# Two slots of 160 for an expert's last whole slot and its rest, with a projection and weight loads moved, in a two-layer gated cross-attention kernel

## The chip, the core and the metric

The kernel runs on one core of a Trainium2 chip. The metric is the device time of one execution in microseconds (us). The core's engines work side by side, each on its own in-order queue: TensorE (PE) multiplies, with its weight loads shown as a row of their own (PEld); VectorE (DVE) and ScalarE (ACT) work on elements; GpSimd (POOL) does the rest of the element work and issues the gathers and scatters by index; SyncE (SP) issues nearly all other transfers. Waits between queues go by semaphores. The profile also shows the clock that TensorE was granted, as a share of full speed.

## The reference, cut to what matters

Two layers; each adds a cross-attention and a mixture of experts to x (8 batches of 100 tokens, 512 features). All is float32.

```
x = x + tanh(g_xattn[0]) * L0_xattn(ctx, layernorm(x), mask)
x = x + tanh(g_ffn[0])   * L0_ffn(layernorm(x))
x = x + tanh(g_xattn[1]) * L1_xattn(layernorm(x), ctx)
x = x + tanh(g_ffn[1])   * L1_ffn(layernorm(x))

L0_ffn:  4 experts, 2048 hidden, the two best by softmax probability
    logits = x @ router_w + router_b
    out = sum over the token's experts e of gate[t, e] * (silu(x @ w1[e]) * (x @ w3[e])) @ w2[e]
L1_ffn:  8 experts, 1024 hidden, the two best by logit, gates by their softmax
    the same with W1, W2, W3
```

Layer 0's attention has latents from x and keys and values from a masked context of 722 tokens and the latents; 16 heads of 64. Layer 1's attention reads every 16th key of the context's projection; 16 heads of 32. So 1600 token-expert pairs go through each mixture, and how many fall to each expert is known only when the router has run.

## The kernel before, in words

**Layer 0's attention** has two forms, and the kernel branches between them at run time: `attend_to_all`, and `attend_to_few` where no pair of batches has more than 128 usable context tokens. These inputs take the second, called the arm below. Ahead of the branch run the masks' running counts (`cum`, written to DRAM as `cum_d`) and the first latents; the largest count is read into a register, and each engine branches on it. In the arm, `bring` loads a pair's counts back to all partitions, `find` turns them into row indices on VectorE, `fetch` gathers the context rows, and `Pair.steps` builds queries (`wq`), values (`wv`) and keys (`wk`). The loop over the four pairs weighs one pair's heads (`softmax`, `weigh`, `finish`) and between them runs steps of a list `fill`: the next pair's projections, the earlier pair's output projection, routers, and in the last pair the first half of layer 1's keys and values (`kv`) and the choice of layer 0's first expert (`First.find`, one stage for each `c`). The stages end in 24 tiny matmuls (`pe_f`, L542) that put the first slot's rows in order.

**A mixture** works in slots: one expert's weights times up to 256 tokens. The first slot takes up to 256 tokens of the expert that is most wanted among the early batches (6 of layer 0, 5 of layer 1), so it can start before the router has seen all. Its rows come from `First`: `begin_rows` issues the gathers on POOL, `begin_weights` reads the expert's number into a register of SP and issues the weights, 1 MB each: w1 and w3 (up) and w2 (down) for each group of 512 hidden features; three buffers of each. While the first slot runs, `steps` runs between its products: what is left of the attention (`last_outputs`: the output projections of batches 6 and 7; two steps of it ahead of the slot), the routers of the late batches, and `dispatch`, the plan for all other tokens: counts per expert, minus what the first slot took, cut into whole slots of 256 and a rest. `SLOTS` says how many slots of each size there are: `(n_mid, n128, always, n256, middle)`. A rest of at most 128 goes into one of the n128 slots, one up to `middle` (192 in layer 0, 160 in layer 1) into one of the n_mid, a larger one into a whole slot, and so does whatever no longer fits. The first `always` whole slots run unconditionally, further ones each behind a branch. The order is: middle slots, slots of 128, whole slots. `slot` multiplies with w1 and w3 (L1564), gates on ScalarE and VectorE, and multiplies with w2, turned for a middle slot (L1536, results transposed back in the next slot, L1601) and straight for the others (L1547); `before_last` transposes the next slot's gathered rows (L1510) between the last two down products.

**Layer 1's attention** runs batch by batch; its router of a batch follows one batch behind (`route`), and `First.find` runs its stages in the last two batches. `mix.begin_weights(2)` loads w1 and w3 as soon as the expert is known; the rest follows at the end of the loop.

The code is traced in program order; a scheduler then orders each engine's queue by what is ready in its own estimate, and adds the semaphores. `issue_after` holds the instructions of its block behind one instruction on that one's engine.

Of the kernel before, what the change touches and what calls it, by code (L numbers as in the profile page):

```python
# [42 lines left out]

WHOLE = 2 * P
# [4 lines left out]
SLOTS1 = (2, 4, 3, (2 * NT - 2 * EARLY1 * S // E1 + E1 * (WHOLE - 1)) // WHOLE, 160)  # L49
# [14 lines left out]
def flamingo_gated(  # L64
# [84 lines left out]
    def load_kv0(pool, bufs, order):  # L149

        wkv_r = wkv0.rearrange("(kc p) n -> p kc n", p=P)
        tiles = {}
        for k, i in enumerate(order):
            t = pool.tile([P, KC, 512], FP, tag=("wk", "wv")[i // 2], name="wkv", bufs=bufs)
            nc.sync.dma_start(t, wkv_r[:, :, bass.ts(i, 512)])
            tiles[i] = t
            if k == 1:
                load_x(2, 3)
        return [tiles[0], tiles[1]], [tiles[2], tiles[3]]
# [101 lines left out]
    with ExitStack() as ph:  # L261
        ps_c = ph.enter_context(tc.tile_pool(name="p_ps", bufs=1, space=PSUM))
        nc.vector.tensor_copy(cum, m8)

        nc.vector.tensor_tensor_scan(cum, cum, cum, 0.0, ALU.add, ALU.max)
        pm = ps_c.tile([1, 512], FP, name="pm")
        nc.tensor.transpose(
            pm[:, :PAIRS], cum[:, 2 * CTX - 1 : 2 * CTX], ident[:PAIRS, :PAIRS]
        )
        top = prep.tile([1, 1], FP, name="top")  # L270
        nc.vector.tensor_reduce(top, pm[:, :PAIRS], AX.X, ALU.max)
        nc.vector.tensor_copy(most, top)
        nc.gpsimd.dma_start(cum_d, cum)
    prep.release()
# [18 lines left out]
    def project_out(b, ps, tag, work, y_tag="y", y_bufs=1):  # L293
        oT = oT0[:, :, bass.ts(b % 2, S)]
        py = ps.tile([P, 512], FP, tag=tag, name="py")
        for c in range(IN0 // P):
            nc.tensor.matmul(
                py[:S],
                oT[:, c, :],
                wo[:, c, :],  # L300
                start=(c == 0),
                stop=(c == IN0 // P - 1),
            )
        add_normed(b, py, work, y_tag, y_bufs)

# [164 lines left out]
    class First:  # L470
# [3 lines left out]
        def __init__(self, E, early, lg, gates, t_gate):  # L474
            self.E, self.early, self.lg, self.gates, self.t_gate = E, early, lg, gates, t_gate
            self.rows = state.tile([P, 2], I32, name=f"f_rows{E}")
            self.gate = state.tile([P, 2], FP, name=f"f_gate{E}")
            self.e = state.tile([1, 1], I32, name=f"f_e{E}")
            self.taken = state.tile([P, E], FP, name=f"f_taken{E}")

        def find(self, space, ps, tag):
# [58 lines left out]
            for t in range(2):  # L540
                for k in range(b):
                    nc.tensor.matmul(  # L542
                        pe[:, bass.ts(t, 2)], place[:, k, bass.ts(t, P)], what[:, k],
                        start=(k == 0), stop=(k == b - 1),
                    )
# [7 lines left out]
            v.scalar_tensor_tensor(self.rows, both[:, :, 0], -1.0, free, ALU.add, ALU.add)  # L553
# [47 lines left out]
    def load_heads(pool):  # L601
# [4 lines left out]
        def load(c, kc):  # L606
            if kc < 2:
                t = pool.tile([P, KC, 512], FP, tag="wv", name="ch", bufs=2)
# [11 lines left out]
    def attend_to_all():  # L620
# [210 lines left out]
        wk, wv = load_kv0(kvp, 2, (0, 1, 2, 3))  # L831
# [3 lines left out]
        for b in range(B):  # L835
# [5 lines left out]
            for hf in range(2):  # L841
# [16 lines left out]
                if hf == 0:  # L858
                    v = v_next
            if b < EARLY0:  # L860
                project_out(b, ps_mm, "mm", work, "o", 2)
# [4 lines left out]
        for _, step in keys_values_1(  # L866
# [7 lines left out]
            load_heads(kvp),  # L874
# [5 lines left out]
    def attend_to_few():  # L880
# [264 lines left out]
        space = bring(0, pair.kT)  # L1145
        wk, wv = load_kv0(kvp, 2, (2, 3, 0, 1))
        load_rest()
        find(0, space)
        pair.fetch()
        pair.norm_context()  # L1150
        for k, (_, step) in enumerate(pair.steps()):
# [13 lines left out]
            load_heads(kvp),  # L1165
# [3 lines left out]
        for i in range(PAIRS):  # L1169
# [11 lines left out]
            else:  # L1181
# [6 lines left out]
                fill += [c, kv[3], kv[4], c, c, kv[5], c, c, kv[6], c, kv[7], c]  # L1188
# [19 lines left out]
            for c in range(n):  # L1208
                now = softmax(pair, c)
                while done < len(fill) and cost < whole * (c + 1) / n:  # L1210
# [5 lines left out]
                last = now  # L1216
            finish(*last)
# [39 lines left out]
    def dispatch(E, slots, first, wk_, ps_pool):  # L1257
# [6 lines left out]
        n = base + 2 * n256  # L1264
        v = nc.vector
# [52 lines left out]
        v.tensor_tensor(put[:, 0], put[:, 0], put[:, 1], ALU.subtract)  # L1318
        ends = vec("ends", 3)
# [4 lines left out]
        for k, have in ((0, n_mid), (1, n128)):  # L1324
# [3 lines left out]
            v.tensor_tensor(put[:, k], put[:, k], fit[:, 0], ALU.mult)  # L1328
        apart = vec("apart")
        v.tensor_tensor(apart[:, 0], put[:, 0], put[:, 1], ALU.add)  # L1330
        yield
# [9 lines left out]
        v.tensor_scalar(rest[:, 0], ends[:, 0], 2.0, -2.0, ALU.mult, ALU.add)  # L1341
        v.tensor_tensor(rest[:, 0], rest[:, 0], put[:, 0], ALU.mult)
# [27 lines left out]
        v.tensor_tensor(far, far, grid(main), ALU.add)  # L1370
        v.tensor_tensor(at2[:, 0], at2[:, 0], far, ALU.add)
        yield
# [73 lines left out]
    class Mixture:  # L1446
# [38 lines left out]
        def begin_weights(self, upto=3):  # L1485

            if not self.w0:
                self.e = self.expert(self.first.e[0:1, 0:1])
# [233 lines left out]
    def last_outputs(ps, work):  # L1722
        for b in range(EARLY0, B):
# [29 lines left out]
    mix.run(last_outputs, range(EARLY0, B), 2, 1, between, ending)  # L1753
# [5 lines left out]
    with ExitStack() as ph:  # L1759
# [161 lines left out]
        for b in range(B):  # L1921
# [5 lines left out]
            if b:  # L1927
                logits = route(
                    b - 1, ps_t, "t", wk_, wg, lg1, out, nc.scalar.copy, nc.sync
                )  # L1930
# [8 lines left out]
            project_1(b, oT)  # L1939
# [86 lines left out]
```

## Time and profile before

| what | us |
|---|---|
| median of 3 runs (1433.77 to 1436.92) | 1436.36 |
| the profiled execution | 1435.67 |
| its span, first to last instruction | 1433.9 |
| the branch is left on POOL, VectorE (first instruction behind it) | 16.96, 20.11 |
| first queries, first values on PE | 17.44, 33.57 |
| last weighing in layer 0's attention ends | 390.97 |
| first product of layer 0's first slot | 415.21 |
| first product of layer 1's first slot | 1098.90 |
| first slot of 160, of 128, of 256 of layer 1 begins | 1148.76, 1204.85, 1292.56 |
| last product ends | 1418.4 |

The span is cut on the page into 40 slices of 35.85 us. Page rows give an engine's busy share; a row of the timeline reads: start, length, engine, line, operation, output<-inputs, shapes, count, and in brackets the engine's idle time just before and what released it ("issue": nothing that the profile shows). The mean granted clock is 0.982 over the span.

### The profile page before, as it was taken

How to read it: one execution, taken by the hardware profiler on the slowest of the kernel's cores; microseconds unless marked ns; L12 is line 12 of the kernel's file. 1: busy time of each engine (PE TensorE's matmuls, PEld its weight loads, DVE VectorE, ACT ScalarE, POOL GpSimd, SP SyncE). 2: the span in 40 equal slices, each digit the busy share in tenths (PEclk: the TensorE clock that was granted, in tenths of full speed). 3: DMA queues.
4: the chain of work that ended last, by engine and by line, in shares of the span. 5: the costliest groups of instructions: out<-in, count | busy, mean ns of one | idle time of the engine just before them, and what ended most of it. 6: DMA issues, size and time to landing. Idle time of an engine off the chain costs nothing. (4 is left out here: it accounts for less than half of the span.)

```text
span 1433.9 us, 18211 instructions
## 1 busy us (share of the span) xinstructions
PE 1371.5 (96%) x7077; PEld 1024.5 (71%) x7077; DVE 479.4 (33%) x1357; ACT 251.7 (18%) x727; POOL 185.5 (13%) x277
## 2 busy tenths in 40 slices
PE   4999999999999999999999999998998999999995
PEld 3566857767568699997677777764666799787773
DVE  4353654535735121222121212113574423222220
ACT  1124423234311000100000000002542001010000
POOL 3410201100120100010000000005211111110000
PEclk9999999999999999999999999998997999999998
DMA  8400101111296466664355526422015578885521
GB/s 274 128 1 0 41 6 35 60 33 44 106 334 235 140 218 226 205 221 157 125 170 176 191 91 218 138 83 62 24 47 213 220 265 270 292 304 194 191 45 17
DMA packets 103856, 207.95 MB, mean 145 GB/s; under 512 B 6166, under 2 KB 13338, under 8 KB 103748
## 3 DMA queue, kind: packets, MB, share of 16 engines
q1 hardware_dynamic: 95556, 186.72, 37.1%
q0 software_dynamic: 8192, 19.84, 5.7%
q8 instruction: 61, 1.00, 0.3%
q14 instruction: 47, 0.39, 0.1%
HBM read 191.18 MB, written 15.36 MB: 144 GB/s over the span
## 5 line engine op out<-in xcount | busy, mean ns | idle before, releaser
L1564 PE MATMUL pa<-xTs,w 128*128 128x256 f32 (+3 forms) x1536 | 317.3, 349 | 1.4 <-DVE xTs L1513 1.3
L1564 PE MATMUL pb<-xTs,w 128*128 128x256 f32 (+3 forms) x1536 | 312.9, 347 | 0.0
L1564 PEld LDWEIGHTS pa<-xTs,w 128*128 128x128 f32 x1536 | 262.5, 191 | 33.9 <-issue 9.9
L1564 PEld LDWEIGHTS pb<-xTs,w 128*128 128x128 f32 x1536 | 262.6, 191 | 22.8
L1547 PE MATMUL py_e<-w,hT 128*128 128x512 f32 x512 | 225.7, 593 | 0.0
L1572 ACT ACTIVATE sg<-pa 128x256 f32<-128x256 f32 (+3 forms) x192 | 67.2, 350 | 718.6 <-PE pa L1564 708.9
L1573 DVE TENSOR_TENSOR sg<-sg,pa 128x256 f32<-128x256 f32 (+3 forms) x192 | 72.9, 380 | 345.8 <-ACT sg L1572 345.8
L1547 PEld LDWEIGHTS py_e<-w,hT 128*128 128x128 f32 x512 | 96.2, 191 | 106.4 <-issue 103.6
L1574 DVE TENSOR_TENSOR hT<-sg,pb 128x256 f32<-128x256 f32 (+3 forms) x192 | 72.8, 379 | 124.6 <-PE pb L1564 124.4
L1052 PE MATMUL pv_f<-wkv,kvT 128*100 128x512 f32 (+1 forms) x192 | 87.8, 607 | 3.4 <-DVE qT L1029 3.4
L1038 PE MATMUL pk_f<-kvT,wkv 128*128 128x328 f32 x256 | 73.3, 444 | 1.1 <-ACT kvT L1009 1.0
L1472 POOL DMA_INDIRECT xt<-xnd,rows x26 | 25.5, 982 | 373.6 <-PE pt_s L1510 293.5
L1052 PEld LDWEIGHTS pv_f<-wkv,kvT 128*100 128x100 f32 (+1 forms) x192 | 33.3, 177 | 48.6 <-issue 43.7
L1090 ACT ACTIVATE pr_f<-pr_f,nmax 100x228 f32<-100x228 f32 x128 | 60.7, 475 | 36.5 <-DVE nmax L1080 33.1
L1038 PEld LDWEIGHTS pk_f<-kvT,wkv 128*128 128x128 f32 x256 | 47.9, 190 | 23.9 <-ACT kvT L1009 2.1
L1080 DVE CUSTOM_DVE_ANT_0 pr_f<-ps_sf,bias 100x228 f32<-100x228 f32 x128 | 43.7, 391 | 54.3 <-PE ps_sf L1067 54.1
L1536 PE MATMUL py_e<-hT,w 128*128 128x192 f32 (+1 forms) x384 | 61.0, 318 | 0.0
L1536 PEld LDWEIGHTS py_e<-hT,w 128*128 128x128 f32 x384 | 59.3, 190 | 0.0
L1606 POOL DMA_INDIRECT xr<-ye,rows x12 | 18.7, 1559 | 267.5 <-DVE ye L1605 266.9
L1022 PE MATMUL pq_f<-kvT,wq 128*128 128x200 f32 x256 | 46.4, 342 | 3.0 <-ACT kvT L1009 3.0
L1513 DVE COPY xTs<-pt_s 128x512 f32<-128x512 f32 x30 | 19.7, 687 | 86.7 <-PE pt_s L1510 86.7
L1022 PEld LDWEIGHTS pq_f<-kvT,wq 128*128 128x128 f32 x256 | 44.3, 195 | 4.3 <-ACT kvT L1009 4.0
(353 smaller groups left out, 1203.2 us busy)
## 6 DMA issues: line engine op xcount, KB each, us to landing
w<-in_f_w_dram SPq DMA_DIRECT2D x144, 1024.0 KB
ch<-in_ctx_heads_dram SPq DMA_DIRECT2D x12, 720.0 KB
wkv<-in_wkv_dram SPq DMA_DIRECT2D x4, 1024.0 KB
kT<-cum_d SPq DMA_DIRECT2D x4, 722.0 KB
wq<-in_ctx_heads_dram SPq DMA_DIRECT2D x4, 720.0 KB
wq<-in_wq_dram SPq DMA_DIRECT2D x4, 512.0 KB
wo<-in_wo_dram SPq DMA_DIRECT2D x1, 2048.0 KB
xnd<-xn POOLq DMA_DIRECT2D x9, 200.0 KB, 4.6
```

Of the source, the lines that this page charges most:

```text
L1022: nc.tensor.matmul(pq[:, bass.ts(i, 2 * S)].rearrange("p (j s) -> p j s", j=2), wq[:, kc, bass.ts(c0 + i, P)], self.lats[kc], start=(kc == 0),
L1038: nc.tensor.matmul(pk[:, : S + FK], wk[c // 4][:, kc, bass.ts(c % 4, P)], self.kvT[:, kc], start=(kc == 0), stop=(kc == KC - 1),)
L1052: nc.tensor.matmul(pv[:n], self.kvT[:, kc, k0 : k0 + n], wv[hf][:, kc, :], start=(kc == 0), stop=(kc == KC - 1),)
L1080: nc.vector.tensor_tensor_reduce(out=pr[:, r, j], in0=ps[:S, r, bass.ts(j, FK)], in1=p.bias[j], scale=-1.0, scalar=FMAX, op0=ALU.add, op1= ...
L1090: nc.scalar.activation(pr[:, r, j], pr[:, r, j], AF.Exp, bias=nmax, scale=-1.0, accum_out=sm[:, r, j : j + 1],)
L1472: nc.gpsimd.indirect_dma_start(out=xt, out_offset=None, in_=xnd[: LEAD + upto * S], in_offset=bass.IndirectOffsetOnAxis(ap=rows[:, k : k + ...
L1536: nc.tensor.matmul(pys[c // 2][:, bass.ts(c % 2, T)], w2[:, i, bass.ts(c, P)], hT[:, i, :T], start=False, stop=(fg == F // FG - 1 and i == ...
L1547: nc.tensor.matmul(py[:n], hT[:, i, c : c + n], w2[:, i, :], start=(fg == 0 and i == 0), stop=(fg == F // FG - 1 and i == FG // P - 1),)
L1564: nc.tensor.matmul(p[:, :T], w[:, kc, bass.ts(i, P)], xT[:, kc, :T], start=(kc == 0), stop=(kc == KC - 1),)
L1572: nc.scalar.activation(sg[:, :T], pa[:, :T], AF.Sigmoid)
L1573: nc.vector.tensor_tensor(sg[:, :T], sg[:, :T], pa[:, :T], ALU.mult)
L1574: nc.vector.tensor_tensor(hT[:, i, :T], sg[:, :T], pb[:, :T], ALU.mult)
```

## The change

It has six parts.

- `SLOTS1` is (4, 3, 2, n256, 160) instead of (2, 4, 3, n256, 160), and `dispatch` learns to split: where an expert has a whole slot and a rest of at most 2 x (middle - 128) tokens (64 in layer 1, 128 in layer 0) and two middle slots are free, its last whole slot and the rest go into two middle slots. It costs some VectorE operations and one more stage.
- The output projection of batch 6 leaves the mixture's first slot and goes into the arms. In the arm of these inputs `project_parts` cuts it at chunks 3 and 6: the first piece before the last stage but one of the choice, the second before the last head pair is finished, the third behind it. Of the stages one call less stands in `fill`; the rest of the choice runs behind the third piece. The mixture runs one step instead of two ahead of its first slot.
- The two value weights of layer 0's attention (`wv`) and the first pair's running counts (into `wo`'s space, `cum0`) are loaded ahead of the branch, in the order wv0, cum0, wv1; then, inside the arm, the first pair's `find` and `fetch`, the two `wk`, x of batches 2 and 3, and the rest.
- The first slot's expert number is copied a second time (`e_late`) behind its rows, and the second `begin_weights` of layer 1 reads that copy.
- In the last batch of layer 1's attention the rows of batch 6 are normalized first; router 6 and projection 7 go behind the last of the choice's tiny matmuls (`counted`) on PE.
- Layer 1's chunk loads take the `wv` tiles themselves instead of new tiles of that tag.

```diff
-SLOTS1 = (2, 4, 3, (2 * NT - 2 * EARLY1 * S // E1 + E1 * (WHOLE - 1)) // WHOLE, 160)
+SLOTS1 = (4, 3, 2, (2 * NT - 2 * EARLY1 * S // E1 + E1 * (WHOLE - 1)) // WHOLE, 160)
...
+    def load_kv0(pool, tag, i, bufs=1):
+
+        t = pool.tile([P, KC, 512], FP, tag=tag, name="wkv", bufs=bufs)
+        nc.sync.dma_start(t, wkv_r[:, :, bass.ts(i, 512)])
+        return t
...
         nc.gpsimd.dma_start(cum_d, cum)
+
+        cum0 = wo.rearrange("p c n -> p (c n)")[:, : 2 * CTX]
+        wv = [load_kv0(wpool, "wv0", 2)]
+        nc.sync.dma_start(cum0, cum_d[0].partition_broadcast(P))
+        wv.append(load_kv0(wpool, "wv1", 3))
     prep.release()
     few = nc.values_load(most, min_val=0, max_val=2 * CTX)
...
+    def project_parts(b, cuts, ps, tag, work, y_tag="y", y_bufs=1):
+
+        n = IN0 // P
         py = ps.tile([P, 512], FP, tag=tag, name="py")
-        for c in range(IN0 // P):
+        for c in range(n):
+            if c in cuts:
+                yield
             nc.tensor.matmul(
...
-            v.scalar_tensor_tensor(self.rows, both[:, :, 0], -1.0, free, ALU.add, ALU.add)
+            known = v.scalar_tensor_tensor(
+                self.rows, both[:, :, 0], -1.0, free, ALU.add, ALU.add
+            )
+            with tc.issue_after(known.ins):
+                v.tensor_copy(self.e_late, number)
...
         pair = Pair(0)
-        space = bring(0, pair.kT)
-        wk, wv = load_kv0(kvp, 2, (2, 3, 0, 1))
+        find(0, cum0)
+        pair.fetch()
+        wk = [load_kv0(kvp, "wk", i, 2) for i in range(2)]
+        load_x(2, 3)
         load_rest()
-        find(0, space)
-        pair.fetch()
...
-                fill += [c, kv[3], kv[4], c, c, kv[5], c, c, kv[6], c, kv[7], c]
+                fill += [c, kv[3], kv[4], c, c, kv[5], c, kv[6], c, kv[7], c]
...
                 now = softmax(pair, c)
-                while done < len(fill) and cost < whole * (c + 1) / n:
+                if following is None and c == n - 1:
+
+                    parts = project_parts(EARLY0, (3, n - 2), ps_mm, "mm", work)
+                    fill.insert(-1, (0, lambda: next(parts)))
+                while done < len(fill) and (cost < whole * (c + 1) / n or c == n - 1):
...
+            if following is None:
+                next(parts)
+                finish(*last)
+                next(parts, None)
+                for _ in choice:
+                    pass
+                break
...
+        over_ = middle - P
...
+        two = vec("two")
+        v.tensor_scalar(two[:, 0], left[:, 0], float(2 * over_), None, ALU.is_le)
+        v.tensor_tensor(two[:, 0], two[:, 0], some[:, 0], ALU.mult)
+        had = vec("had")
+        v.tensor_scalar(had[:, 0], q[:, 0], 0.0, None, ALU.is_gt)
+        v.tensor_tensor(two[:, 0], two[:, 0], had[:, 0], ALU.mult)
+        v.scalar_tensor_tensor(put[:, 0], two[:, 0], 2.0, put[:, 0], ALU.mult, ALU.add)
...
+            if not k:
+                v.tensor_tensor(two[:, 0], two[:, 0], fit[:, 0], ALU.mult)
+                v.tensor_tensor(put[:, 1], put[:, 1], two[:, 0], ALU.subtract)
+                v.tensor_tensor(q, q, two, ALU.subtract)
         apart = vec("apart")
         v.tensor_tensor(apart[:, 0], put[:, 0], put[:, 1], ALU.add)
+        v.tensor_tensor(apart, apart, two, ALU.subtract)
...
+        yield
+        v.scalar_tensor_tensor(row, grid(q), -2.0, at2[:, 0], ALU.mult, ALU.add)
         v.tensor_tensor(at2[:, 0], at2[:, 0], far, ALU.add)
+        turns = wk_.tile([S, 2, B, E], FP, tag="pick", name="turns")
+        for t in range(2):
+            v.tensor_scalar(turns[:, t], row, float(1 + t), None, ALU.is_equal)
+            v.tensor_tensor(turns[:, t], turns[:, t], grid(two), ALU.mult)
+        v.tensor_tensor(at2[:, 0], at2[:, 0], turns[:, 0], ALU.add)
+        v.tensor_tensor(at2[:, 0], at2[:, 0], turns[:, 1], ALU.subtract)
+        v.tensor_scalar(row, at2[:, 1], float(over_), None, ALU.is_ge)
+        v.tensor_tensor(row, row, turns[:, 1], ALU.mult)
+        v.scalar_tensor_tensor(at2[:, 0], row, 2.0, at2[:, 0], ALU.mult, ALU.add)
+        v.scalar_tensor_tensor(at2[:, 1], row, -float(over_), at2[:, 1], ALU.mult, ALU.add)
...
-            if not self.w0:
-                self.e = self.expert(self.first.e[0:1, 0:1])
+            self.e = self.expert((self.first.e_late if self.w0 else self.first.e)[0:1, 0:1])
...
-        for b in range(EARLY0, B):
+        for b in range(EARLY0 + 1, B):
             project_out(b, ps, "m", work)
...
-    mix.run(last_outputs, range(EARLY0, B), 2, 1, between, ending)
+    mix.run(last_outputs, range(EARLY0, B), 1, 1, between, ending)
...
-            if b:
-                logits = route(
-                    b - 1, ps_t, "t", wk_, wg, lg1, out, nc.scalar.copy, nc.sync
-                )
+            how = (ps_t, "t", wk_, wg, lg1, out, nc.scalar.copy, nc.sync)
+            if b > EARLY1 + 1:
+                xn = norm_rows(b - 1, wk_, out, nc.sync)
+            elif b:
+                logits = route(b - 1, *how)
...
                 next(find)
-            project_1(b, oT)
+                with tc.issue_after(first1.counted.ins):
+                    logits = route(b - 1, *how, xn)
+                    project_1(b, oT)
+            else:
+                project_1(b, oT)
```

## The prediction

> **What bounds the kernel now.** First the page's busy times and its slices: is one engine full, and where not.
>
> ```profile
> span 1433.9 us, 18211 instructions
> PE 1371.5 (96%) x7077; PEld 1024.5 (71%) x7077; DVE 479.4 (33%) x1357; ACT 251.7 (18%) x727; POOL 185.5 (13%) x277
> ...
> PE   4999999999999999999999999998998999999995
> ```
>
> TensorE (PE) is full but for the two ends and a dip near slice 28. Time can be won by giving PE less to do, or at its few waits. Then the stretches of layer 1's slots, cut where the chain of waits changes from one slot to the next; each row gives a stretch's length, busy times, granted clock, DMA share and GB/s:
>
> ```profile
> 1148.76:1176.58 27.82, 27.82 (x203) 27.18 (x203) 7.18 (x19) 2.85 (x9) 3.57 (x3) 1.00 0.70 230
> 1176.58:1204.85 28.27, 28.27 (x209) 27.76 (x209) 7.72 (x20) 2.85 (x9) 3.99 (x3) 1.00 0.75 246
> 1204.85:1227.32 22.47, 22.47 (x158) 18.56 (x158) 7.19 (x20) 2.22 (x8) 3.91 (x3) 1.00 0.85 294
> 1227.32:1248.92 21.60, 21.60 (x151) 17.74 (x150) 6.06 (x18) 2.22 (x8) 2.57 (x2) 1.00 0.91 316
> ...
> 1334.79:1377.03 42.24, 42.24 (x170) 31.30 (x169) 9.53 (x20) 3.06 (x8) 3.08 (x2) 1.00 0.44 134
> ```
>
> Two slots of 160, two of 128, one of 256: PE is busy throughout, so a slot's length is its PE work. Last the timeline at the seams, where PE waits. Around the end of layer 0's attention arm:
>
> ```profile
> 387.00 0.56 PE L1122 MATMUL po_f<-cT,v 128*64 128x200 f32 x4 [1.67 <-ACT cT L1119]
> ...
> 390.90 5.28 PE L542 MATMUL pe_f<-space 100*128 100x2 f32 x24
> ...
> 396.54 15.38 PE L297 MATMUL py<-wo,oT 128*100 128x512 f32 x32 [0.35 <-DVE space L548]
> ...
> 411.75 0.60 PE L1510 MATMUL pt_s<-ident,xt 128*128 128x128 f32 x4
> ```
>
> and at the start of layer 1's mixture:
>
> ```profile
> 1085.59 2.31 PE L542 MATMUL pe_f<-xT 100*128 100x2 f32 x20
> ...
> 1088.78 1.10 POOL L1472 DMA_INDIRECT xt<-xnd,f_rows  x1 [4.29 <-DMA w<-in_f_w_dram]
> ...
> 1095.36 1.09 PE L1510 MATMUL pt_s<-ident,xt 128*128 128x128 f32 x4 [3.82 <-DMA xt<-xnd,f_rows]
> ...
> 1098.90 3.78 PE L1564 MATMUL pa<-xTs,w 128*128 128x256 f32 x8
> ```
>
> At the first seam PE goes straight on into the two late output projections (py, 32 matmuls); at the second it waits 3.82 us for the gathered rows, and its first 8 products then take 3.78 us, where later ones take 1.73.
>
> **Part 1, the slots.** Which slots run hangs on the data. Evaluating the reference's second router on its inputs gives 239, 98, 255, 130, 129, 125, 294 and 330 tokens for the eight experts; the first slot takes 225 of the last, leaving 105. Today that is two slots of 160 (130, 129), four of 128 (98, 125, 105, and the 38 behind 294's whole slot) and three of 256 (239, 255, 294): the sizes that the trace shows, with nothing in the conditional slots. After, the 294 go into two of 160 (256 + 38, and 38 is under 64): four of 160, three of 128, two of 256, again exactly what is unconditional. Added: two slots of 160. One that follows and precedes another costs 28.27 + 0.43 (it turns two gathered tiles for its successor, where the row's slot turns one; four transposes are half of the 0.87 us that eight take) = 28.70. Taken away: 21.60 and 42.24. So 2 x 28.70 - 21.60 - 42.24 = **-6.4 us**. The slots load as many weights as before, nine times 6 MB; the longest run of short ones becomes three of 128 (DMA share 0.91 in such a slot) where it was four, so DMA does not step in. Layer 0's counts (186, 253, 162, 231 left, two of them behind a whole slot) call for no split: its slots stay.
>
> **Part 2, the plan costs more VectorE work.** About 11 narrow operations (128x8) and 11 wide (100x64) come in, and the plan is asked for one step later. In the first slot 54 such operations took 6.0 us (1111.14 to 1117.16), 0.11 each; a wide one that waits for its predecessor took about 0.24 (L1369 at 1116.32, L1370 at 1116.55). 1.2 + 2.6 = 3.9 us later. What hides it: the last plan row is ready at 1128.9, the second gather is issued at 1130.59 and lands 7.1 later (median of these gathers), 1137.7, and PE wants it at 1140.85, so 3.15 are spare. I take 3.9 - 3.15 = **+0.7**; from 0 (gathers land in 3.3 at best) to +3 (a gather at 8.2, interleaving with the slot's own products). What is late then is the transposing for the second slot. In layer 0 the plan is ready at 471.4 in a first slot that lasts to about 500; nothing there.
>
> **Part 3, output projection 6 moves into the arm** and is cut in three, the last piece behind the last head's weighing. PE does the same 16 matmuls (half of 13.75 at full clock), but may do them where it waited: 1.67 + 0.64 us between 385 and 390. The clock matters more. The stretches 385 to 400, in fives, show a granted clock of 0.92, 0.50 and 0.56. At full clock the 24 tiny matmuls would take 24 x 0.115 = 2.8 (the row at 1085.59) against 5.28, the two projections 13.75 against 15.38, the weighing 1.08 against 1.82: 2.5 + 1.6 + 0.7 = 4.8. Together 7.1, so the first slot's transposes at 404.6 instead of 411.75. Against this: the rows are known only when the tiny matmuls end, and in the arm they may now queue behind pieces of the projection, to about 397.5; gathers at 398.5 and 399.8, the second landing by 406.9. VectorE and POOL get the projection's normalization (0.70 + 0.18 + 0.75 + 0.75, and 0.8 on POOL) ahead of the rows in program order, and the weights of the first slot (issued at 397.05) may wait for its buffers; three of them need some 8 us. These covers end at about 407 to 409, when PE, at 404.6 plus the 3.46 from transposes to first product, would ask. I take **-5.5**, from -2.3 (idle filled, clock not won) to -7.1.
>
> [...]
>
> **Part 4, layer 1's head.** The tiny matmuls come ahead of router 6 and projection 7: place is ready at 1083.76, they started at 1085.59, so rows and gathers are 1.7 us earlier. The load of w2 and the next weights now waits for a copy behind the rows (e_late); behind it on SP's queue stand w2 and the second group's weights, moved from 1086.05 to about 1088. 3 MB at the 390 GB/s of that stretch take 8 us and land by 1098; the second group is wanted after 1113: covered. That leaves the gathers less crowded. With the second issued at 1088.5 and landing in 3.3 (best) to 7.1 (median) us, against 1097.0 today: -1.4 to -5.2; and up to 2.05 more (3.78 - 1.73) if PE does not cool in between. Middle landing -3.3, half of the clock: **-4.3**, from -1.4 to -7.2.
>
> **Part 5, loads ahead of the branch.** wv0, the running counts (cum0) and wv1 go onto SP's queue before the branch; SP waits there for cum_d to be written, and wv1, its own branch, wk, x and wo stand behind that wait.
>
> ```profile
> 13.72 0.35 SPq L895 DMA_DIRECT2D kT<-cum_d  x1
> ...
> 20.11 0.16 DVE L904 MEMSET at<- 128x1 f32 x4 [5.41 <-issue]
> ...
> 30.53 0.69 DVE L236 BATCH_NORM_STATS2 st<-ct 128x6 f32<-128x512 f32 x1 [7.57 <-DMA ct<-in_ctx_dram,index]
> ...
> 33.57 15.67 PE L1052 MATMUL pv_f<-wkv,kvT 128*100 128x512 f32 x32 [3.43 <-DVE qT L1029]
> ```
>
> The counts cannot be read before 13.72 either way; VectorE comes out of the branch at 20.11, after 5.41 us without a named wait, and that, not the load, holds the index. Weights are needed at 33.57 (wv) and 50.2 (wk), long after they land. So nothing on the path moves: **0**, from -3.4 (a less crowded fetch of ct ends PE's 3.43 us wait) to +4 (the rival below).
>
> **The sum:** -6.4 + 0.7 - 5.5 - 4.3 + 0 = -15.5. The profiled run took 1435.67 (span 1433.9 and 1.77 around it), 0.69 under the median of the runs: 1435.67 - 15.5 = 1420.2, on the median 1420.9. I say 1420.5.
>
> **Rivals.**
> *The seams give little* (25%): the projection's tail takes the place of the wait removed, the clock stays low, the gathers still land in 7.1. -6.4 + 1.5 - 2.3 - 1.4: 1427.5. For it: VectorE is busy 4.84 of 5 us before 390, and the clock was still 0.56 from 395 to 400, under dense projections. Against: the pieces have no late input but the last.
> *All of it* (14%): -6.4 - 7.1 - 7.2 - 3: about 1412.5.
> *A slower entry into the arm* (9%): queued weight loads hold up what the engines fetch at the branch. VectorE's 5.41 and POOL's 3.30 us without a named wait stand there with DMA loading; PE waited 6.62 us so, in a stretch where DMA went idle (share 0.03 at 12 to 14 us), and PE would now meet wv0. 4 us (between 3.3 and 5.41) later: 1424.5. Against: it has from 8.1 to 14.6 for it. [...]
> *A conditional slot opens* (5%), the slower side: if the split does not do what it says, or any class of experts is miscounted, a whole slot more runs behind a branch, with nothing loaded ahead. 42.2 for it and 7.2 for its first weights (the load at 1081.54 in the chain) make 49: about 1470. It decides from four tokens: expert 5 with 129 instead of 125 would need a fifth slot of 160. Against: the counts fit exactly today too.
> *No change* (2%): the seams lose what the slots win.
>
> **Numbers.** My forecast 45%. 80% range 1411 to 1430: it takes in all but the last two rivals and the far ends. 0.2% (2.9 us) is about what can be told from no change. Faster is the first four cases but a hundredth of the seams case that the other two parts could eat up: 0.92; same 0.03; slower 0.05.
>
> **What would show it.** In layer 1 four slots of about 28.5, three of 22, two of 42 us, no slot behind them. The first product of layer 0's mixture at about 409.5 (was 415.21), with 16 projection matmuls ahead of it and 0.9 or more of granted clock from 385 on; that of layer 1's, counted from the last projection, 4 us sooner, the gather 1.7 us behind the tiny matmuls' earlier end. Values still start near 33.6. I am wrong if projection 6 leaves PE waiting for VectorE or weights in the arm, if the second slot waits over 3 us for its rows, or if the entry moves by over 3 us.

## The result, and the profile after

| | us, median (runs) | against before |
|---|---|---|
| before | 1436.48 (1432.18 to 1438.44, 20) | |
| after | 1431.24 (1425.72 to 1438.52, 20) | 0.9972, 95% interval 0.9960 to 0.9984 |
| after, once more (e12) | 1432.12 (1428.56 to 1435.47, 12) | 0.9968, 0.9955 to 0.9980 |

Faster, but by 4 to 5 us where 15.5 were forecast; 1431.24 is also above the forecast's range. First the page of the kernel after, its span, PE's busy time and PE's slices:

```profile
span 1429.4 us, 18472 instructions
...
PE 1362.0 (95%) x7181; PEld 1027.8 (72%) x7181; DVE 485.8 (34%) x1405; ACT 252.3 (18%) x729; POOL 189.4 (13%) x279
...
PE   4999999999979999999999999998998999999995
```

PE does 9.5 us less work than before (1371.5), but the span is shorter by 4.5 only, and slice 12, around 410 us, shows a dip (7) that was not there: some of the saved work came back as waiting. The stretches of layer 1's slots (length, busy times, granted clock, DMA share, GB/s), the second and third slot of 160, two of 128 and the first of 256:

```profile
1177.88:1206.58 28.70, 28.70 (x211) 28.01 (x211) 8.32 (x21) 2.86 (x9) 4.99 (x4) 1.00 0.74 255
1206.58:1235.28 28.70, 28.70 (x211) 28.01 (x211) 8.32 (x21) 2.86 (x9) 4.98 (x4) 1.00 0.75 246
...
1263.55:1286.09 22.54, 22.54 (x159) 18.62 (x158) 7.20 (x20) 2.22 (x8) 3.92 (x3) 1.00 0.83 290
1286.09:1307.69 21.60, 21.60 (x150) 17.73 (x150) 6.05 (x18) 2.22 (x8) 2.58 (x2) 1.00 0.89 318
...
1329.72:1371.95 42.23, 42.23 (x169) 31.23 (x169) 9.53 (x20) 3.08 (x8) 3.10 (x2) 1.00 0.47 161
```

The two slots that came in take the forecast 28.70 each, and no conditional slot ran. The dip is at the end of the arm. The timeline of the kernel after there:

```profile
391.39 2.74 PE L549 MATMUL pe_f<-space 100*128 100x2 f32 x24
...
394.56 0.16 DVE L560 SCALAR_TENSOR_TENSOR f_rows<-space 128x2 int32<-128x2 f32 x1
...
397.89 1.96 PE L302 MATMUL py<-wo,oT 128*100 128x512 f32 x4 [0.59 <-ACT oT L1217]
...
401.74 7.08 PE L302 MATMUL py<-wo,oT 128*100 128x512 f32 x16 [1.88 <-DVE y L362]
401.76 1.26 POOL L365 TENSOR_TENSOR x<-x,ob 100x512 f32<-100x512 f32 x1
401.81 1.75 DVE L366 SCALAR_TENSOR_TENSOR x<-y,mv,x 100x512 f32<-100x512 f32 x1 [0.22 <-POOL mv L240]
403.83 1.56 SPq L1276 DMA_DIRECT2D w<-in_f_w_dram  x3
404.43 1.11 POOL L1526 DMA_INDIRECT xt<-xnd,f_rows  x1 [1.41 <-issue]
...
412.07 0.63 PE L1563 MATMUL pt_s<-ident,xt 128*128 128x128 f32 x4 [3.25 <-issue]
...
415.39 3.78 PE L1617 MATMUL pa<-xTs,w 128*128 128x256 f32 x8 [0.80 <-DVE xTs L1566]
...
418.96 2.57 PE L1617 MATMUL pb<-xTs,w 128*128 128x256 f32 x8
```

The tiny matmuls run at full clock (2.74 us, granted clock 1.00 from 390 to 395) and the rows are known at 394.72, two us before the kernel before had them. But the gather that reads them is issued at 404.43 and the weights at 403.83: not behind the rows, but behind projection 6's last step on VectorE, which ends at 403.56. PE waits for projection 6's buffer on VectorE (1.88, one of the prediction's own signs of being wrong) and then 3.25 us more, where the row names no releaser but the gathers landed 7.0 us after their issue; and after this the first two groups are slow, 3.78 and 2.57 us (granted clock 0.50 from 415 to 420), where before took 2.00 and 1.89 (1.00).

Every profile of this study can be cut at four marks: the first context rows in the arm (first statistics on `ct`), the second group of w1 products in layer 0's first slot, the first `pkv` near that mixture's end (550.12 or 550.13 us later in each), and the begin of layer 1's first slot of 160; the last stretch goes to the end of the last product:

| us | before | after | forecast change | measured change | after again (e12) |
|---|---|---|---|---|---|
| first context rows | 30.53 | 31.88 | 0 | +1.35 | 32.40 |
| to the second group (first seam) | 388.58 | 389.84 | -5.5 | +1.26 | 394.19 |
| from `pkv` to the first slot of 160 (head and plan) | 179.45 | 178.22 | -3.6 | -1.23 | 177.83 |
| layer 1's slots | 269.70 | 263.26 | -6.4 | -6.44 | 263.26 |

### The profile page after: what moved, and what is told of

It reads as the page before. It is cut to its first block, busy times and chain, and to the rows that moved or that the text cites. A ratio compares the mean times of both kernels' runs of the same rounds, so it can differ in the third digit from the quotient of the medians.

```text
span 1429.4 us, 18472 instructions
## 1 busy us (share of the span) xinstructions
PE 1362.0 (95%) x7181; PEld 1027.8 (72%) x7181; DVE 485.8 (34%) x1405; ACT 252.3 (18%) x729; POOL 189.4 (13%) x279
## 5 line engine op out<-in xcount | busy, mean ns | idle before, releaser
L1617 PE MATMUL pb<-xTs,w 128*128 128x256 f32 (+3 forms) x1536 | 309.8, 344 | 0.0
L1600 PE MATMUL py_e<-w,hT 128*128 128x512 f32 x464 | 204.4, 592 | 0.0
L1600 PEld LDWEIGHTS py_e<-w,hT 128*128 128x128 f32 x464 | 87.1, 190 | 97.0 <-issue 94.7
L1589 PE MATMUL py_e<-hT,w 128*128 128x192 f32 (+1 forms) x512 | 79.0, 313 | 0.0
L1589 PEld LDWEIGHTS py_e<-hT,w 128*128 128x128 f32 x512 | 76.8, 190 | 0.0
```

Source lines behind the costliest of these rows:

```text
L1589: nc.tensor.matmul(pys[c // 2][:, bass.ts(c % 2, T)], w2[:, i, bass.ts(c, P)], hT[:, i, :T], start=False, stop=(fg == F // FG - 1 and i == ...
L1600: nc.tensor.matmul(py[:n], hT[:, i, c : c + n], w2[:, i, :], start=(fg == 0 and i == 0), stop=(fg == F // FG - 1 and i == FG // P - 1),)
L1617: nc.tensor.matmul(p[:, :T], w[:, kc, bass.ts(i, P)], xT[:, kc, :T], start=(kc == 0), stop=(kc == KC - 1),)
```

## The experiments

Each was run with its own runs of the kernel before; ratios are against those (medians 1435.54 to 1436.15). "Seam" is the second row of the table above.

**e1**: the kernel after with projection 6 back behind the arm (part 3 undone).

```diff
-            if following is None:
-                next(parts)
-                finish(*last)
...
-        for b in range(EARLY0 + 1, B):
+        for b in range(EARLY0, B):
...
-    mix.run(last_outputs, range(EARLY0, B), 1, 1, between, ending)
+    mix.run(last_outputs, range(EARLY0, B), 2, 1, between, ending)
```

> The changed kernel with projection 6 back in the first slot of layer 0's mixture (part 3 undone, all else kept). My theory: the arm ends as one unit, so POOL's gathers and SP's weight loads for the first slot stand behind projection 6's normalization; that cost the first seam some 1.8 us and about 1 more behind it, which now comes back. The gathers are issued within 1.5 us of the rows again, first product about 415.9 without a cold start, and the time is 2 to 4 us under the changed kernel: 1427.5 to 1429.5. Rival: the seam was lost to something else at the branch's end (loads ahead of the branch, another buffer layout), then the gathers stay some 9 us behind the rows and the time stays at 1431.

1429.47 us (6 runs), 0.9951 (0.9936 to 0.9966): without the part that should bring 5.5, the kernel is no slower. Its gather is issued at 401.36, 0.92 behind the rows. **e2** is the kernel before with `SLOTS1` and `dispatch` alone.

> The kernel before with the new slots and the new plan alone (parts 1 and 2). My theory: the stretch from the end of layer 1's first slot to the last product falls from 269.6 to 263.2 us, the first slot itself grows by 0.4 by the longer plan: -6.0 in all, 1430.5. Rival: more slots of 160 ask for weights faster than DMA brings them or their results queue on POOL, and part of the 6 us is given back at the end: -3, 1433.5.

1428.09 us (6 runs), 0.9952 (0.9935 to 0.9968). Slots and plan alone give at least as much as the whole change: 3 us more by the medians, though the intervals overlap. **e3** is the kernel before with part 3 alone.

> The kernel before with projection 6 moved into the arm alone (part 3). My theory: slower by 1.8 to 3 us, 1438 to 1439.5, with the gathers some 9 us behind the rows though PE's clock stays full to 410. Rival, my forecast's own: the moved products fill PE's waits and win the clock, -5.5: 1431.

1439.81 us (12 runs), 1.0025 (1.0011 to 1.0040): by the ratio it is slower than before by 3.6 us. Its profile has the picture of the kernel after: rows known at 395.34, the last normalization step 406.22 to 407.97, weights at 408.24, gather at 408.84; seam 394.47.

**e4**: the kernel after, but projection 6 ends in the arm with one copy of its raw result (into columns of `oT0` that are free by then); its normalization stands behind the arm, after the gathers.

```diff
+        if b == EARLY0:
+            nc.vector.tensor_copy(held, py[:S].rearrange("p (c n) -> p c n", n=64))
+            return
         add_normed(b, py, work, y_tag, y_bufs)
...
+        add_held(EARLY0, work)
         for b in range(EARLY0 + 1, B):
```

> The changed kernel, but the arm ends projection 6 with one VectorE copy of the raw result into SBUF (batch 6's own columns of oT0); its normalization runs behind the arm, after the first slot's gathers and loads are issued. My theory: gathers within 3 us of the rows instead of 9.7, projection 7 no longer waits 1.9 us for its PSUM buffer, first product at about 410.5 instead of 415.4 and no cold start: 5 to 7 us under the changed kernel, 1424 to 1426. Rival: the arm's end holds POOL and SP whatever stands in it last (VectorE's copy is as good a barrier), and only 1 to 2 us come back: 1429.5.

1427.9 us (7 runs), 0.9949 (0.9929 to 0.9969). Rows known at 396.00, copy on VectorE 405.00 to 405.69, weights at 405.95, gather at 406.55: again 0.26 and 0.86 behind VectorE's last instruction, whatever it is. Seam 388.7. The rival had the gather right. **e8** is e4 with that copy on ScalarE (`nc.scalar.copy`).

> As e4 (projection 6 ends in the arm with one copy of its raw result, the normalization stands behind the arm), with that copy on ScalarE instead of VectorE. Theory: a gather behind the arm waits for the arm's whole VectorE part, 0.87 us behind its last instruction, because it waits on VectorE for its rows; without the copy on VectorE that last instruction is the gate's or the rows' own, so the gather is issued about 0.9 after them (near 396.8 where rows are at 395.9) and the first product comes 4 us or more sooner than e4's 416.99, up to where other waits stand. Rival: the arm ends as a unit whichever engine is last, the gather stays about 0.9 behind the copy's end near 405.7, and the time is that of e4, 1427.9.

1425.05 us (6 runs), 0.9924 (0.9907 to 0.9942), seam 384.35. Both expectations missed the gather: it was issued at 400.18, neither 0.9 behind the rows (392.78) nor near 406. The run that repeats it (**e13**, the same kernel) shows what it does follow:

> e8 once more (the changed kernel with projection 6's raw result copied by ScalarE at the arm's end, its normalization behind the arm). Theory: the stretch from the first context rows to the second group of layer 0's first slot is 382 to 385 again, some 5 us under that of e12, and the median is 3 to 6 us under e12's. Rival: e8's 1425.05 was a lucky set of executions; the median is within 2 us of e12's.

1425.36 us (6 runs), 0.9936 (0.9917 to 0.9955), beside **e12**, the kernel after again:

> The changed kernel itself, once more, beside e13. From the profiles so far the time is a sum: arrival of the first context rows (30.1 to 33.1 us, by the execution), from there to the second group of layer 0's first slot (389.84 in the changed kernel's profile), then 550.12, then 178.2 up to layer 1's first slot of 160, then 263.26. Theory: the second of these belongs to the kernel, because the gather waits for the normalization: again between 388 and 393, median 1429 to 1433. Rival: it belongs to the execution's clock; it may be under 386 or over 395 here.

1432.12 us, 0.9968 (0.9955 to 0.9980). Side by side on one chip the mended tail is worth 4.6 us by the ratios and 6.8 by the medians. The timeline of e13:

```profile
372.65 1.29 POOL L383 TENSOR_TENSOR x<-x,ob 100x512 f32<-100x512 f32 x1
...
395.11 0.16 DVE L578 SCALAR_TENSOR_TENSOR f_rows<-space 128x2 int32<-128x2 f32 x1
...
398.44 1.96 PE L303 MATMUL py<-wo,oT 128*100 128x512 f32 x4 [0.59 <-ACT oT L1235]
...
400.50 0.59 ACT L307 COPY oT<-py 100x512 f32<-100x512 f32 x1 [2.10 <-PE py L303]
400.61 1.56 SPq L1294 DMA_DIRECT2D w<-in_f_w_dram  x3
...
401.13 7.11 PE L303 MATMUL py<-wo,oT 128*100 128x512 f32 x16 [0.73 <-ACT oT L307]
401.18 1.29 POOL L1544 DMA_INDIRECT xt<-xnd,f_rows  x1 [26.01 <-ACT oT L307]
...
408.27 0.63 PE L1581 MATMUL pt_s<-ident,xt 128*128 128x128 f32 x4
...
411.59 1.99 PE L1635 MATMUL pa<-xTs,w 128*128 128x256 f32 x8 [1.26 <-DVE xTs L1584]
```

PE's last product of the arm ends at 400.40 and the weights go out 0.21 later, before ScalarE's copy has ended; the gather 0.78 later, 0.09 behind the copy. So the gather and the weights still come only behind the arm's last product, 5 us behind the rows, but the normalization is no longer in the arm. Whether the gather follows that product or ScalarE's copy, these rows do not tell. They do tell that the branch does not hold the engines: POOL's addition for batch 6 (L383) stands behind the branch in the program and ran at 372.65, 28 us before the arm's last product ended; in the kernel after, PE's projection 7 (401.74) and POOL's addition (401.76) began before VectorE had done the arm's last step. Only the gather and the loads wait. PE goes from py (ending 408.24) straight to the gathered rows, and the first group takes 1.99. From the projection's third piece to the first group PE waited 0.59 + 0.73 + 0.79 + 1.26 = 3.4 us here, 0.59 + 1.88 + 3.25 + 0.78 + 0.80 = 7.3 in the kernel after.

**e11** asks for the cause alone: the slots-only kernel (e2) with four operations on VectorE as the last of the arm, whose results nothing reads.

```diff
+        for _ in range(4):
+            nc.vector.tensor_scalar(
+                work.tile([P, 512], FP, tag="pr", name="idle"), wo[:, 0, :], first0.gate[:, 0:1], None, ALU.mult
+            )
```

> The slots alone (e2), with four operations on VectorE added as the last of the arm (128x512 into a scratch tile that nothing reads; they need the first slot's gates, so they stand behind the rows). Nothing that they make is used. Theory: POOL's gather and SP's weights behind the arm wait for the arm's whole VectorE part, so they are issued 0.87 and 0.27 us behind the last of these operations' ends, some 2.2 to 2.8 us later than in e2 (397.33 and about 396.7), while the rows are known at 396.3 as in e2. Rival: they wait for the rows alone; the gather stays about 1.0 behind them, near 397.3. The time itself should move by no more than 1 us, since PE asks for the rows only near 411.

The timeline of e11:

```profile
398.47 0.16 DVE L553 SCALAR_TENSOR_TENSOR f_rows<-space 128x2 int32<-128x2 f32 x1
398.55 1.67 DVE L1235 TENSOR_SCALAR idle<-wo,f_gate 128x512 f32<-128x512 f32 x4
...
400.49 2.10 SPq L1256 DMA_DIRECT2D w<-in_f_w_dram  x3
401.09 1.06 POOL L1506 DMA_INDIRECT xt<-xnd,f_rows  x1 [26.23 <-DVE idle L1235]
```

The idle work ends at 400.22; weights 0.27, gather 0.87 later, the same two numbers as behind the rows before, behind the normalization after and in e3, and within 0.01 of those behind the copy in e4. In e2, without the idle work, the gather came 0.86 behind the rows' end. So the gather and the weights wait for the arm's last work on VectorE, whether or not they need it: this is shown by itself. What ties them to it is not shown. The arm's buffers are given back at its end (`ph.close()`), and the pools for gathered rows and weights are opened behind it; a wait for that space is one candidate, a wait that covers an engine's whole arm is another, and no run takes the two apart. The time (1436.27, one run) was not within 1 us as expected, but 8 over e2's median: its first context rows came 1.7 later, its seam was 390.39 against 389.01 (its projections also waited 1.14 us, by their row for the idle work), and its layer 1 head took 3.2 more; one run cannot say which of these belong to it.

**e5** is the kernel after with the loads behind the branch again (part 5 undone), **e7** the kernel after with the first pair's copy of the counts on VectorE instead of ScalarE:

```diff
-            nc.scalar.copy(
+            (nc.scalar.copy if i else nc.vector.tensor_copy)(
```

> The changed kernel with part 5 alone undone: the loads of wv and of the counts stand behind the branch again. Theory: the changed kernel's late start (values on PE at 35.91 us where before had 33.57) is the price of part 5, so first queries come at about 17.5 and values at about 33.6 again, everything behind is as in the changed kernel, and the time falls by about 2 us: 1429. Rival: the start moves with something else of the change or with the execution (code size, the clock), values stay at about 35.5 and the time at 1431.

> The changed kernel with one instruction on another engine: the first pair's copy of the counts, which waits for their load, goes to VectorE instead of ScalarE. Theory: the late start is that copy standing on ScalarE ahead of the latents' activations (10.92 us of wait until 17.67), so queries begin at about 17.5 instead of 19.56, values at 34 to 34.5 instead of 35.9, and the time falls by 1.5 to 2 us. Rival: the late start is the entry into the arm under load (first transposes at 15.86 with 7.59 us without a named wait), so values stay above 35 and the time moves by no more than 0.5.

e5: 1429.3 us (9 runs), 0.9956 (0.9941 to 0.9970); values at 33.61. e7: 1434.55 (12 runs), 0.9987 (0.9972 to 1.0001). e5 came out as expected, but e9 against e8 (below) undoes the same part and came out 2.9 us slower. The copy's theory fell: queries started 0.84 sooner (18.72), values later (38.82), and the time did not fall. Its profile has the longest seam of all (397.47). 3.5 us of that lie before the first values, which come 7.53 us behind the first context rows where the kernel after has 4.03: VectorE normalizes those rows before it copies the queries, PE waits 4.35 us for that copy, and the last 16 query products take 4.66 us where they took 2.97. What sets the start shows in the rows of the entry, here of the kernel after:

```profile
18.52 0.55 POOL L997 MEMSET bias<- 100x100 f32 x4 [4.71 <-issue]
19.17 0.16 DVE L917 MEMSET at<- 128x1 f32 x4 [4.32 <-issue]
23.98 1.13 POOL L962 DMA_INDIRECT ct<-in_ctx_dram,index  x1 [1.89 <-issue]
31.88 0.69 DVE L233 BATCH_NORM_STATS2 st<-ct 128x6 f32<-128x512 f32 x1 [10.56 <-DMA ct<-in_ctx_dram,index]
```

and of e10 (below), which has no part 5:

```profile
19.86 0.54 POOL L1006 MEMSET bias<- 100x100 f32 x4 [6.11 <-issue]
20.69 0.16 DVE L926 MEMSET at<- 128x1 f32 x4 [5.91 <-issue]
25.92 1.13 POOL L971 DMA_INDIRECT ct<-in_ctx_dram,index  x1 [2.51 <-issue]
32.99 0.69 DVE L237 BATCH_NORM_STATS2 st<-ct 128x6 f32<-128x512 f32 x1 [8.71 <-DMA ct<-in_ctx_dram,index]
```

The arm runs at a nearly fixed pace behind the first context rows: one set of scores (`ps_sf`) near 348 us begins 317.0 to 317.3 us behind them in ten profiles, 315.6 to 316.8 in after, e8 and e9, 318.2 in e13 and 320.3 in e7. In the rows shown they land when VectorE and POOL have come out of the branch (2.6 to 6.5 us without a named wait, over the profiles) and the gather has gone through. It is not so in every execution: in e12 and e4, both with part 5, VectorE was out earliest of all (17.43 and 17.66) and then waited 3.89 and 3.77 us for the counts, whose load SP had issued only at 15.47 and 15.65 (13.29 in the kernel after); their context rows are among the latest, at 32.40 and 32.19. With part 5 they were there at 30.1 to 33.1 us (seven profiles, mean 31.7), without it at 30.1 to 33.0 (eight, mean 31.1): the part makes no difference in the mean that stands out of this spread.

**e6** is the kernel before with slots, plan and head, without parts 3 and 5. **e9** is e8 without part 5, **e10** is e9 without the head.

> The kernel before with the slots of part 1, the plan of part 2 and layer 1's head of part 4; projection 6 stays behind the arm (no part 3) and the loads behind the branch (no part 5). Theory: the head wins what its two profiles showed, 1 to 2.7 us, beside the slots alone (1428.1): 1425.5 to 1427; gather of layer 1's first rows some 2 us nearer to the attention's end than before. Rival: the tiny matmuls ahead of projection 7 run at half clock and wait for place on VectorE, which eats it: 1428 or more.

> e8 (projection 6 ends in the arm with one raw copy on ScalarE) with part 5 undone, so slots, plan, projection and head, but the loads behind the branch. Theory: the gains add up, since the start (values back at 33.6 instead of 34.15) and the first seam do not touch: 1425.05 less about 1.5 to 2, so 1423 to 1423.5, values at 33.6, gather within 1.0 us of the last projection product in the arm. Rival: they do not add up, because the place in time where the clock is lowered moves with the start; 1425 or more, with a granted clock under 0.9 between 395 and 405.

> The kernel before with the slots and the plan (parts 1 and 2) and projection 6 in the arm with the raw copy on ScalarE; neither the head of layer 1 nor the loads ahead of the branch. It tells what part 4 is worth behind a good first seam. Theory, from e2 and e6 (1428.09 and 1429.49): the head wins nothing that the runs can tell, so this is within 2 us of e9, 1422 to 1425, with the gather of layer 1 as before some 1.7 us later behind the attention but the tiny matmuls at full clock. Rival: the head wins the 2 to 2.7 us that the two profiles show, and this is over e9 by that, 1425 to 1426.

e6: 1429.49 us (5 runs), 0.9962 (0.9947 to 0.9976). e9: 1427.96 (6 runs, 1421.42 to 1431.67), 0.9951 (0.9936 to 0.9967). e10: 1428.02 (6 runs), 0.9952 (0.9935 to 0.9968). The seams of e9 and e10 are as short as e8's (381.98 and 383.96), but their medians are within 0.2 us of e2's. So "the gains add up" did not come out; the rival's time did, but not its sign: e9's granted clock between 390 and 420 was 1.00 throughout in its profile. That profile is the fastest of its six executions, 1421.42 us with a span of 1419.7 and a mean granted clock of 0.989; the five others had 0.981 to 0.988, the two slowest (1430.41 and 1431.67) 0.981 and 0.983, so most of what they lost goes with the clock. Where in the kernel it was lost is not to be seen. e10's profile lost 2.9 us against e2's by its late first context rows. The head shows in no median: e6 against e2 is 1.4 us slower with it (its rival came out), e9 against e10 the same within 0.1. And e5 against e6, with and without part 3 as changed, differs by 0.2 us in the medians, where e3 had that part 3.6 slower.

All profiles, by the first seam:

| projection 6 | seam, us |
|---|---|
| behind the arm (before, e1, e2, e6; e11 with its idle work) | 388.6, 390.5, 389.0, 390.4; 390.4 |
| in the arm as changed (after, e12, e3, e5, e7) | 389.8, 394.2, 394.5, 391.5, 397.5 |
| in the arm, raw copy on VectorE (e4) | 388.7 |
| in the arm, raw copy on ScalarE (e8, e13, e9, e10) | 384.4, 384.4, 382.0, 384.0 |

Two things are mixed here, the kernel and the clock. From the begin of the tiny matmuls to the end of projection 6's third piece the ten kernels with it in the arm ask PE for the same work; it took 8.5 us in after, e9, e10 and e13 (granted clock 1.00 from 390 to 405), 10.0 and 10.1 in e8 and e5, and 12.7 in e3, e4, e7 and e12 (0.50 in the middle of it). At like clock the normalization costs about 5.5 us: 389.8 against 384.4 (after, e13), 394.2 against 388.7 (e12, e4). So e4's copy on VectorE is as good as e13's on ScalarE, but for the clock. In the five with projection 6 behind the arm the clock was at 0.50 to 0.60 from 390 to 395 each time.

The best version is e8 (e13): ratio 0.992 to 0.994, 5 to 7 us under the kernel after.

## Why the prediction was wrong

**Part 1, the slots, was right**: -6.4 forecast, -6.44 measured (269.70 to 263.26, and 263.26 or 263.27 wherever I measured the new slots). **Part 2, the plan, was nearly so**: +0.7 forecast; e2 against before shows +0.23 in the head's stretch, which is within what that stretch varies (179.5 to 180.6 in the four without the head), and PE did not wait ahead of the second slot.

**Part 3 is the step that failed**: -5.5 forecast, and a mean of +3.9 measured (seams of 393.5 over five profiles with it, 389.6 over four without); by the ratios +3.6 us (e3 against before), +2.4 and +3.0 (e12 and after against e1) and -0.9 (e5 against e6). What the prediction put wrong is first one clause: "the rows are known only when the tiny matmuls end [...] gathers at 398.5 and 399.8", with covers that end "at about 407 to 409". The rows came earlier than that (394.72), PE's tiny matmuls at 2.74 as forecast, and the idle of 1.67 was filled. But the gathers came at 404.43 and 405.84, since they and the weights follow the arm's last work on VectorE (by 0.87 and 0.27 us here) or, where VectorE is done before, come only behind PE's last product (0.78 and 0.21 in e13), not behind the rows alone. In the kernel before the rows were that last work, so the profile before could not tell the two apart:

```profile
396.62 0.16 DVE L553 SCALAR_TENSOR_TENSOR f_rows<-space 128x2 int32<-128x2 f32 x1
397.05 2.42 SPq L1252 DMA_DIRECT2D w<-in_f_w_dram  x3
...
397.65 1.06 POOL L1472 DMA_INDIRECT xt<-xnd,f_rows  x1 [24.11 <-DVE f_rows L553]
```

I had the normalization's 0.70 + 0.18 + 0.75 + 0.75 us in view and took it for something that is late itself, not for what the first gather and loads behind the arm wait for. That costs about 5.5 us at like clock. The second step is the clock: 4.8 of the part's 7.1 us were to come from it, and of the five profiles with the part only one kept it at 1.00 through the arm; the slow arm costs 4.3. With the normalization taken out of the arm and the clock high (e8, e9, e10 and e13, mean 383.7) the seam is 5.9 us shorter than in the four without the part, about the forecast's size; with the clock low (e4, 388.7) it is 0.9 shorter. The medians give less: e8 and e13 are 4 us under e1, e9 is 1.5 under e6, and e10 equals e2. So the part can bring what was forecast, but only where the clock stays high, and the arm does not ensure that: e4's and e13's are the same up to the copy. As far as these runs tell, the clock was luck of the execution.

One us of that end looks like a collision. The last step took 1.75 us (401.81 to 403.56) beside POOL's addition for batch 7 (401.76 to 403.02); the same operation took 0.74 us at 415.25, with POOL idle. The addition began first, and 0.54 us of the step lie behind its end. The step took 1.75 or 1.76 us in all five profiles where the two meet (after, e3, e5, e7, e12) and 0.75 in e4, e8, e9, e10 and e13, where the addition had run before; no run moves the addition alone, so more than this meeting is not shown.

**Part 4, the head, was mis-sized**: -4.3 forecast, and with the plan's +0.7 a net -3.6; measured -1.2 in the two profiles, and -1.7 as a mean (178.2 over ten profiles with it, 177.1 to 181.0; 180.0 over before, e2, e3 and e10, without e11's 182.9). The medians do not show it (e6 against e2, e9 against e10). The timeline of the kernel after:

```profile
1086.22 4.39 PE L549 MATMUL pe_f<-xT 100*128 100x2 f32 x20 [1.77 <-DVE xT L541]
...
1091.49 1.11 POOL L1526 DMA_INDIRECT xt<-xnd,f_rows  x1 [4.69 <-DMA w<-in_f_w_dram]
...
1100.12 0.66 PE L1563 MATMUL pt_s<-ident,xt 128*128 128x128 f32 x4 [1.28 <-DMA xt<-xnd,f_rows]
...
1101.56 1.99 PE L1617 MATMUL pa<-xTs,w 128*128 128x256 f32 x8 [0.78 <-DVE xTs L1566]
```

Counted from `pkv`, the tiny matmuls begin 1.97 us sooner (114.38, before 116.35), as forecast. But they now wait 1.77 us for VectorE, run at half clock (0.59 and 0.50 from 1085 to 1095) and take 4.39 where they took 2.31, so the gather is issued no sooner (119.65, 119.54) and the first group begins no sooner (129.72, 129.66). So the step that failed here is the 1.7 us earlier gather, and what was won is the other half of the term: that group at 1.99 instead of 3.78. PE now has router 6 and projection 7 where it waited, and the granted clock from 1095 to 1105 is 0.88 and 1.00 where it was 0.50 and 0.74. That half was also sized a little too high: 3.78 is a length and 1.73 a step between two starts; a later group's length is 1.89, so at most 1.9 was to be had, not 2.05. What lowers the granted clock at this head, no run takes apart.

**Part 5 was right within its spread**: 0 forecast, means 0.6 apart with 3 us of spread on either side. But its reason, that the way out of the branch and not the load holds the index, fails in e12 and e4, where the counts came last. **The rivals**: "the seams give little" was the nearest in kind, and still short: it had the projection's tail take the place of the wait and the slow clock stay, at +1.5 and -2.3 for plan and projection, but not a projection that costs time by itself. The slower entry (+4) is what single executions show, with part 5 and without. That queued loads hold up something that the engines fetch at the branch, no run shows: while VectorE came out of it the queues of kind "instruction" moved three packets in the profile before (14.70 to 20.11) and two in the one after (14.85 to 19.17), and with part 5 VectorE's time without a named wait was 4.32 us against 5.41, POOL's 4.71 against 3.30. No conditional slot opened.

## What to carry to other kernels

Work moved to the end of a run-time arm is not judged by its own result's due time: ask what the first gather and load behind the arm come behind, which here was the arm's last work on VectorE, or on PE where that ended later. Leave the arm's end to what the code behind it really needs, and put the rest (here a normalization) behind the first gather and load. When a profile's last instruction happens to be the operand too, the trace cannot show which of the two is waited for; four idle operations can. And a gain that rests on the clock needs more than one profile: compare stretches of the same work first, and kernels only at like clock.

## What the hardware showed unexpectedly

- SP issued the first loads behind the arm 0.26 to 0.27 us and POOL the gather 0.86 to 0.87 us after VectorE's last instruction of the arm in before, after, e2, e3, e4 and e11 (the gather also in e12), whether they read its result or not (e11).
- The granted clock in one and the same stretch of the kernel moves between executions: the five-microsecond stretches from 395 to 405 show 1.00 and 1.00 in the first profile of the kernel after, 0.50 and 0.52 in the second, with the third piece of projection 6 taking 1.96 and 3.71 us. PE's busy time from 375 up to 395 was 19.98 of 20 us in both, so no idle time stood ahead of the fall in the second, which came as the 24 tiny matmuls ran (392.22 to 395.21; 0.95 from 390 to 395). The runs of this one kernel span 13 us, and most of that goes with the clock: 1425.72 us at a mean granted clock of 0.988, 1438.52 at 0.979, with the 18 others in between.
